# Two layernorm steps, the halved down factor and the planner's hold in a macaron block

## The chip, the cores and the metric

The kernel runs on one core of one Trainium2 chip. The metric is the device time of one execution in microseconds, as a median over runs. The engines of a core work side by side, each through its own list of instructions: TensorE (PE in the profile; its weight loads are PEld), VectorE (DVE), ScalarE (ACT), GpSimd (POOL) and SyncE (SP), which here issues nearly all DMAs.

## The reference

A macaron block in float32: half a gated feed-forward step, causal attention with rotary positions, and the same feed-forward step again. x is 4 x 1024 x 256.

```python
def ffn(x):
    g = (x @ gate_w.T) * gate_s            # 256 -> 704
    u = (x @ up_w.T) * up_s
    return ((silu(g) * u) @ down_w.T) * down_s

x = x + 0.5 * ffn(layernorm(x))
x = x + attn(layernorm(x))                 # 16 heads of 16, rotary, causal softmax
x = x + 0.5 * ffn(layernorm(x))
```

The layernorm has no weights of its own: (x - mean) / sqrt(var + 1e-5). The factor 0.5 ahead of each feed-forward step is folded into its weights.

## The kernel before

**Tiling.** The 4096 rows of x are cut into 8 blocks of 512 rows (two to a sequence), a block into 4 tiles of 128 rows. A block goes through `ffn(i, 1)`, `qkv(i)`, attention and `ffn(i, 2)`. Weights stay in SBUF; the blocks of x stay in six buffers and are updated in place.

**Layernorm.** `norm` (line 334) works on two tiles at a time. VectorE takes the statistics (L339, L342), GpSimd forms the reciprocal root (L348, L349), VectorE the shift (L352, a scalar-tensor-tensor step on two columns), and the tile itself is scaled and shifted by ScalarE (L359) or, for the second tile of each pair of the very first layernorm alone (`dve = [False, src is x0 and i == 0]`), by VectorE (L357): two VectorE tiles in the whole program. For block 0 before its first feed-forward step and its attention, and for the last block before its second feed-forward step, the tiles are then transposed on TensorE (L420) and copied out by ScalarE (L424); all others are transposed by VectorE (L391) and a trip through DRAM (L401, L407).

**Feed-forward.** 22 products of 512 columns give gate and up parts (L466, input wgu); ScalarE's tanh (L480, L500) and VectorE's two steps (L483/L486, L503/L506) give the hidden rows hT; six products for each tile (L526, with wd) go down, and VectorE adds the result to x (L532). A product in float32 is two passes in the trace, so 22 products show as 44 rows.

**The down factor.** wd is scaled on chip by ds = down_s once: `scaled_wd` (line 285) first halves ds (L288), then multiplies each of the six chunks of wd by it (L290), on VectorE, among the first block's steps.

**Fills.** At the start GpSimd writes constants into long-lived buffers (L96 in the profile, `fills` at line 292: hL, padding of wd, three kT, three nm, four va), in between the norms' small steps.

**Attention.** For each block and each pair of head groups, first the row maxima (`max_half`: products L733 into a score buffer, VectorE's mask L756 on the diagonal, and the reduction L789, or L773 where two groups share a buffer), then the maxima are transposed (L813), copied (L816) and sent as an extra row into qT (L821, DMAs on SyncE's queue), then the exponentials (`exp_half`: products L846, ScalarE's L855, GpSimd's masks L867) and the values (`weigh`: L891 into av). L733 and L846 use 16 or 17 of the array's 128 rows, a half two heads and a burst four side by side, a mode that the code calls "row"; L891 uses 32 of the columns, four heads side by side, "col"; all else is "full". Two halves, often one of maxima and one of exponentials, are issued as one *burst*; each has one of two score buffers (att), and a burst needs both free.

**The order.** Nothing is ordered by hand. `Planner` (line 44) holds every operation with an estimated time, keeps a clock for each engine, and at each `step` places the operation that could start earliest; this gives each engine its fixed list of instructions. Bursts compete with the other operations there: a burst is taken if its time, less `WAIT`, comes before that of the best other operation. Its planned time is the longer of its halves plus `CHANGE["row"]` if the mode before was another. After a burst at least `GAP` = 1.2 us of other TensorE work is planned, and values behind full work are put off by `HOLD` = 0.8.

Of the kernel before, what the change touches and what calls it, by code (L numbers as in the profile page):

```python
# [13 lines left out]
ALU = mybir.AluOpType  # L14
# [3 lines left out]
P = 128  # L18
# [25 lines left out]
class Planner:  # L44
# [1 line left out]

    ENGINES = ("pe", "dve", "act", "pool", "dma")
    GAP = 1.2
    WAIT = 0.1
    CHANGE = dict(full=0.2, row=0.2, col=0.12)  # L50
    HOLD = 0.8

# [65 lines left out]
    def step(self, burst):  # L118
        best = None
        for eng in self.ENGINES:  # L120
            for c in self.candidates(eng):
                s = max(c[0], self.busy["pe"] + 0.05) if eng == "pe" else c[0]
                if c[2].mode == "col" and self.mode == "full":
                    s += self.HOLD
                key = (s, c[1])
                if best is None or key < best[0]:
                    best = (key, c)
        b = burst()
        if b is not None:
            at = max(b[0], self.busy["pe"])  # L130
            if self.since < self.GAP:
                at += self.GAP - self.since
            key = (max(at, self.busy["pe"] + 0.05) - self.WAIT, 0)
            if best is None or key < best[0]:
                halves = b[1]
                us = max(h.us for h in halves) + (self.CHANGE["row"] if self.mode != "row" else 0.0)
                at = max(b[0], self.busy["pe"])
                for h in halves:
                    h.us = us
                    self.place(h, at)  # L140
                self.mode, self.since = "row", 0.0
                return b
        assert best is not None, "nothing can be placed"
        (s, _), (at, _, op, q) = best
        if op.eng == "pe":
            self.since += op.us
            if op.mode != self.mode:
                op.us += self.CHANGE[op.mode]
                self.mode = op.mode
        self.place(op, at)  # L150
        if q is not None:
            q.popleft()
        else:
            self.loose[op.eng].remove(op)
        return None
# [15 lines left out]
def tile_macaron(  # L171
# [12 lines left out]
    nc = tc.nc  # L184
    B, T, D = x.shape
# [46 lines left out]
    wd_sb = cpool.tile([P, NI, D], F32, name="wd_sb")  # L232
    gus_sb = cpool.tile([P, 2, NI], F32, name="gus_sb")
    ds_sb = cpool.tile([P, D], F32, name="ds_sb")
# [49 lines left out]

    def scaled_wd(c):

        if c == 0:
            nc.vector.tensor_scalar(ds_sb, ds_sb, 0.5, None, ALU.mult)  # L288
        r = slice(HALF, P) if c == NF else slice(0, P)
        nc.vector.tensor_tensor(wd_sb[r, c, :], wd_sb[r, c, :], ds_sb[r, :], ALU.mult)  # L290

    def fills():

# [16 lines left out]
    wd_loaded = Op("dma", 0.0, lambda: None)  # L310
    gu_loaded.done, wd_loaded.done = 7.5, 16.0
    wd_scaled = [Op("dve", 0.35, partial(scaled_wd, c), [wd_loaded], prio=4) for c in range(NI)]

    xb = [Buf("x") for _ in range(NBLK)]
# [19 lines left out]
    def norm(i, j, src, prio, kind):  # L334

        st, xns = Buf("st"), [Buf(kind), Buf(kind)]

        def stats(n):
            nc.vector.bn_stats(st.tile[:, 6 * n : 6 * n + 6], xb[i].tile[:, j + n, :])  # L339

        def aggr(n):
            nc.vector.bn_aggr(st.tile[:, 12 + 2 * n : 14 + 2 * n], st.tile[:, 6 * n : 6 * n + 6])  # L342

        def of_both(k):
            return st.tile[:, 12:16].rearrange("p (n k) -> p n k", k=2)[:, :, k]

        def power():
            nc.gpsimd.tensor_scalar(st.tile[:, 16:18], of_both(1), EPS, None, ALU.add)  # L348
            nc.gpsimd.tensor_tensor(st.tile[:, 18:20], st.tile[:, 16:18], mhalf, ALU.pow)  # L349

        def shift():
            nc.vector.scalar_tensor_tensor(st.tile[:, 20:22], of_both(0), -1.0, st.tile[:, 18:20], ALU.mult, ALU.mult)  # L352

        def apply(n):
            scale, bias = st.tile[:, 18 + n : 19 + n], st.tile[:, 20 + n : 21 + n]
            if dve[n]:
                nc.vector.tensor_scalar(xns[n].tile, xb[i].tile[:, j + n, :], scale, bias, ALU.mult, ALU.add)  # L357
            else:
                nc.scalar.activation(xns[n].tile, xb[i].tile[:, j + n, :], AF.Identity, bias=bias, scale=scale)  # L359


        dve = [False, src is x0 and i == 0]
        a = [
            Op("dve", 0.35, partial(stats, n), [src[i, j + n]], [st, xns[n]], [xb[i]], prio=prio) for n in range(2)
        ]
        b = [Op("dve", 0.1, partial(aggr, n), [a[n]], uses=[st], prio=prio) for n in range(2)]
        c = Op("pool", 1.0, power, b, uses=[st], prio=prio)
        d = Op("dve", 0.09, shift, [c], uses=[st], prio=prio)
        e = [
            Op(  # L370
                *(("dve", 0.35) if dve[n] else ("act", 0.55)),
                partial(apply, n),
                [d],
                uses=[st, xns[n], xb[i]],
                prio=prio,
            )
            for n in range(2)
        ]
        return a, [*b, c, d, *e], list(zip(xns, e))
# [590 lines left out]
    for blk in range(NBLK):  # L970
        aTs = [Buf("aT") for _ in range(NC)]
        for gs in ((0, 1), (2, 3)):
# [3 lines left out]
            n = len(units) // 2  # L976
# [12 lines left out]
            for i, g in enumerate(gs):  # L989
                us = list(range(n + 1)) if i == 0 else [n + 1, n, *range(n + 2, 2 * n + 1)]  # L990
# [148 lines left out]
```

## Time and profile before

| | us |
|---|---|
| median of 3 runs | 1105.46 (1105.07 to 1106.7) |
| the profiled execution, its own time | 1105.23 |
| its span in the trace | 1103.3 |
| TensorE busy | 1082.3 |
| VectorE busy | 781.7 |
| ScalarE busy | 424.6 |
| GpSimd busy | 255.9 |

The span is what the profile's instructions cover; the profiled execution's own time is 1.9 us longer. The costliest groups on TensorE are L466 (704 passes), L733 and L846 (1536 each), L526 and L891 (1536). In the rows of the profile, an x and a number at the end counts instructions, a `<-` in brackets names what ended an idle time, and times are counted from the start of the span. TensorE's first instruction starts at 7.01, its first product of the feed-forward step at 17.38; the last burst of attention is at 1050.79, and what follows is the last blocks' feed-forward step.

### The profile page before, as it was taken

How to read it: one execution, taken by the hardware profiler on the slowest of the kernel's cores; microseconds unless marked ns; L12 is line 12 of the kernel's file. 1: busy time of each engine (PE TensorE's matmuls, PEld its weight loads, DVE VectorE, ACT ScalarE, POOL GpSimd, SP SyncE). 2: the span in 40 equal slices, each digit the busy share in tenths (PEclk: the TensorE clock that was granted, in tenths of full speed). 3: DMA queues.
4: the chain of work that ended last, by engine and by line, in shares of the span. 5: the costliest groups of instructions: out<-in, count | busy, mean ns of one | idle time of the engine just before them, and what ended most of it. 6: DMA issues, size and time to landing. Idle time of an engine off the chain costs nothing.

```text
span 1103.3 us, 16669 instructions
## 1 busy us (share of the span) xinstructions
PE 1082.3 (98%) x6520; PEld 537.5 (49%) x6520; DVE 781.7 (71%) x1327; ACT 424.6 (38%) x539; POOL 255.9 (23%) x469
## 2 busy tenths in 40 slices
PE   4999999999999999999999999999999999999998
PEld 2646545444454554453544554453635544445365
DVE  6669869668687787667677796677787686675232
ACT  2314333335344344435343353344343343433530
POOL 4132521402021532301103432310214320200110
PEclk9999999999999999999999999999999999999999
DMA  8121200201102012101010011101021010010000
GB/s 274 39 58 32 49 18 20 52 25 42 37 2 58 11 30 49 30 29 48 30 49 26 15 39 28 31 20 39 1 59 30 20 49 1 22 38 20 1 20 19
DMA packets 43132, 40.32 MB, mean 37 GB/s; under 512 B 3952, under 2 KB 35760, under 8 KB 42928
## 3 DMA queue, kind: packets, MB, share of 16 engines
q1 hardware_dynamic: 42912, 39.27, 13.7%
q8 instruction: 51, 0.84, 0.3%
q14 instruction: 25, 0.20, 0.1%
q10 hardware_dynamic: 144, 0.01, 0.0%
HBM read 19.60 MB, written 15.20 MB: 32 GB/s over the span
## 4 chain that ended last, share of the span: by engine, by line
PE 93%; DVE 5%; DMA 1%; SPq 1%; issue 0%; ACT 0%; DVEq 0%
PE d L466 27%; PE att L733 21%; PE d L526 16%; PE av L891 11%; PE att L846 6%; PE d L599 5%; PE d L638 3%; PE d L951 2%; DVE nm L789 1%; DMA wqkv_sb<-in_wqkv 1%; PE d L813 1%; DVE att L756 1%; DVE nm L773 1%; DVE st L339 1%; DVE xs L391 0%
## 5 line engine op out<-in xcount | busy, mean ns | idle before, releaser
L855 ACT ACTIVATE pT<-att 128x1024 f32<-128x1024 f32 x288 | 294.0, 1024 | 482.6 <-PE att L846 482.6
L789 DVE TENSOR_REDUCE nm<-att 128x2 f32<-128x1024 f32 (+1 forms) x320 | 316.3, 1007 | 72.4 <-PE att L846 64.3
L466 PE MATMUL d<-xnT,wgu_sb 128*128 128x512 f32 x704 | 339.2, 611 | 1.2 <-ACT xnT L424 0.7
L733 PE MATMUL att<-kT,qT 16*128 16x512 f32 (+3 forms) x1536 | 316.4, 520 | 2.1 <-DVE nm L773 1.3
L846 PE MATMUL att<-qT,kT 17*128 17x512 f32 (+3 forms) x1536 | 316.4, 520 | 0.0
L867 POOL TENSOR_SCALAR_AFFINE_SELECT pT<-pT 128x256 f32<-128x256 f32 x256 | 99.9, 409 | 494.8 <-ACT pT L855 487.4
L733 PEld LDWEIGHTS att<-kT,qT 16*128 16x128 f32 x1536 | 120.9, 183 | 173.1 <-issue 59.1
L466 PEld LDWEIGHTS d<-xnT,wgu_sb 128*128 128x128 f32 x704 | 124.3, 192 | 159.9 <-issue 135.7
L526 PE MATMUL d<-wd_sb,hT 128*128 128x256 f32 x640 | 162.2, 387 | 0.0
L756 DVE TENSOR_TENSOR att<-att,causal 128x512 f32<-128x512 f32 (+1 forms) x160 | 93.4, 588 | 80.8 <-PE att L846 75.0
L891 PE MATMUL av<-pT,va 128*32 128x512 f32 (+3 forms) x1536 | 137.1, 490 | 0.0
L526 PEld LDWEIGHTS d<-wd_sb,hT 128*128 128x128 f32 x640 | 116.9, 190 | 32.8 <-issue 16.1
L846 PEld LDWEIGHTS att<-qT,kT 17*128 17x128 f32 x1536 | 119.9, 183 | 20.0 <-ACT pT L855 3.0
L503 DVE SCALAR_TENSOR_TENSOR ta<-ta,d 128x512 f32<-128x512 f32 x80 | 54.7, 683 | 53.8 <-ACT ta L500 53.0
L891 PEld LDWEIGHTS av<-pT,va 128*32 128x32 f32 x1536 | 42.7, 109 | 88.2 <-issue 72.3
L500 ACT ACTIVATE ta<-d,gus_sb 128x512 f32<-128x512 f32 x80 | 54.9, 686 | 68.4 <-PE d L466 67.3
L506 DVE SCALAR_TENSOR_TENSOR hT<-d,gus_sb,ta 128x512 f32<-128x512 f32 x80 | 59.6, 744 | 18.6 <-PE d L466 17.7
L599 PE MATMUL d<-xnT,wqkv_sb 128*128 128x512 f32 x128 | 62.6, 606 | 0.0
L610 POOL TENSOR_TENSOR qs<-qs,rope_sb 128x512 f32<-128x512 f32 x32 | 40.7, 1274 | 67.3 <-DVE qs L607 67.2
L348 POOL TENSOR_SCALAR st<-st 128x2 f32<-128x2 f32 x48 | 10.5, 219 | 151.8 <-DVE st L342 145.5
L359 ACT ACTIVATE xn<-x,st 128x256 f32<-128x256 f32 x62 | 34.2, 591 | 28.6 <-DVE st L352 28.0
L532 DVE TENSOR_TENSOR x<-d,x 128x256 f32<-128x256 f32 x64 | 26.7, 418 | 21.8 <-PE d L526 21.3
(57 smaller groups left out, 650.4 us busy)
## 6 DMA issues: line engine op xcount, KB each, us to landing
xd<-xs SPq DMA_DIRECT2D x84, 128.0 KB
xnT<-xd SPq DMA_DIRECT2D x21, 512.0 KB
kT<-qT SPq DMA_DIRECT2D x64, 64.0 KB
out<-x SPq DMA_DIRECT2D x16, 256.0 KB
x<-in_x SPq DMA_DIRECT2D x7, 512.0 KB
qT<-nmT SPq DMA_DIRECT2D x128, 2.0 KB
wgu_sb<-in_wgu SPq DMA_DIRECT2D x2, 512.0 KB
rope_sb<-in_rope SPq DMA_DIRECT2D x1, 1024.0 KB
```

The source lines that it names most:

```text
L466: nc.tensor.matmul(d.tile, wgu_sb[:, k, cols], by_tile(xnT.tile[:, k]), start=(k == 0), stop=(k == NC - 1))
L500: nc.scalar.activation(a.tile, d.tile, AF.Tanh, scale=gus_sb[:, 0, c : c + 1])
L506: nc.vector.scalar_tensor_tensor(hT[c].tile, e.tile, gus_sb[:, 1, c : c + 1], a.tile, ALU.mult, ALU.mult)
L526: nc.tensor.matmul(d.tile[:, :D], hT[c].tile[:, ts(j, P)], wd_sb[:, c, :], start=(n == 0), stop=(n == NI - 1))
L599: nc.tensor.matmul(d.tile, wqkv_sb[:, k, ts(g, P)], xnT.tile[:, k, :], start=(k == 0), stop=(k == NC - 1))
L733: nc.tensor.matmul(sc.tile[:, e, c0 : c0 + w], qT[blk].tile[r, g, ts(j, P)], kt.tile[r, g, :w], start=True, stop=True,)
L756: nc.vector.tensor_tensor(d, d, causal.unsqueeze(1).unsqueeze(1).to_broadcast([P, 2, len(masked), P]), ALU.add)
L789: nc.vector.tensor_reduce(place(g, part, j), sc.tile[:, :, c0 : c0 + w], AX.X, ALU.max, negate=True)
L846: nc.tensor.matmul(sc.tile[:, e, c0 : c0 + w], kt.tile[r, g, ts(k % NB, P)], qT[blk].tile[r, g, BLK - w :], start=True, stop=True,)
L855: nc.scalar.activation(pT.tile[:, :, :w], sc.tile[:, :, :w], AF.Exp)
L867: nc.gpsimd.affine_select(out=d, in_=d, compare_op=ALU.is_ge, fill=0.0, base=0, pattern=[[0, 2], [1, P]], channel_multiplier=-1,)
L891: nc.tensor.matmul(av.tile[ts(r, HP), BLK - w :], va[base + k // NB].tile[:, k % NB, h * VS : h * VS + HP], pTs[u, r // 2].tile[:, r % 2, ...
```

## The change

Three parts. The two VectorE tiles of the first layernorm are written as a scalar-tensor-tensor step, x times scale plus the bias column repeated along the row, in place of a tensor-scalar step with two column operands. The separate halving of ds is dropped, and each of the six scalings of wd is a scalar-tensor-tensor step, wd times 0.5 times ds. In the planner, `WAIT` depends on the mode TensorE is in, 0.3 after values and 0.1 as before elsewhere, and 0.025 is added to every burst's planned time. What is computed is the same.

```diff
     GAP = 1.2
-    WAIT = 0.1
+    WAIT = dict(full=0.1, row=0.1, col=0.3)
     CHANGE = dict(full=0.2, row=0.2, col=0.12)
...
-            key = (max(at, self.busy["pe"] + 0.05) - self.WAIT, 0)
+            key = (max(at, self.busy["pe"] + 0.05) - self.WAIT[self.mode], 0)
             if best is None or key < best[0]:
                 halves = b[1]
-                us = max(h.us for h in halves) + (self.CHANGE["row"] if self.mode != "row" else 0.0)
+                us = max(h.us for h in halves) + 0.025 + (self.CHANGE["row"] if self.mode != "row" else 0.0)
...
     def scaled_wd(c):
 
-        if c == 0:
-            nc.vector.tensor_scalar(ds_sb, ds_sb, 0.5, None, ALU.mult)
         r = slice(HALF, P) if c == NF else slice(0, P)
-        nc.vector.tensor_tensor(wd_sb[r, c, :], wd_sb[r, c, :], ds_sb[r, :], ALU.mult)
+        nc.vector.scalar_tensor_tensor(wd_sb[r, c, :], wd_sb[r, c, :], 0.5, ds_sb[r, :], ALU.mult, ALU.mult)
...
             if dve[n]:
-                nc.vector.tensor_scalar(xns[n].tile, xb[i].tile[:, j + n, :], scale, bias, ALU.mult, ALU.add)
+                nc.vector.scalar_tensor_tensor(
+                    xns[n].tile, xb[i].tile[:, j + n, :], scale, bias.to_broadcast([P, D]), ALU.mult, ALU.add
+                )
```

## The prediction

> **What bounds the kernel now.** First the shares by engine and the chain that ended last (parts 1 and 4 of the page): they say which engine is worth shortening.
>
> ```profile
> PE 1082.3 (98%) x6520; PEld 537.5 (49%) x6520; DVE 781.7 (71%) x1327; ACT 424.6 (38%) x539; POOL 255.9 (23%) x469
> ...
> PE 93%; DVE 5%; DMA 1%; SPq 1%; issue 0%; ACT 0%; DVEq 0%
> ```
>
> TensorE is the bound, and the only one: VectorE has 29% of the span free. Whatever the change does has to show as less work, less switching or less waiting on TensorE. So the next view is the list of TensorE's own waits, longest first (engine, line, releaser: total us, times, longest):
>
> ```profile
> PE d L420 <- DMA wqkv_sb<-in_wqkv: 7.3, 1, 7.3
> PE d L420 <- ACT xn L359: 7.0, 1, 7.0
> PE att L733 <- DVE nm L773: 1.3, 3, 0.5
> PE d L466 <- ACT xnT L424: 0.7, 1, 0.7
> ```
>
> Two waits of 7 us, both before the first product; under 3 us in all the rest. The timeline of the first 28 us (start, us, engine, line, what) tells what they are:
>
> ```profile
> 1.86 1.81 POOL L96 MEMSET kT<- 128x2048 f32 x1
> ...
> 2.93 0.76 DVE L282 TENSOR_SCALAR gus_sb<-gus_sb 128x6 f32<-128x6 f32 x1 [2.93 <-DMA gus_sb<-in_gus]
> ...
> 7.07 3.55 POOL L96 MEMSET kT<- 128x2048 f32 x2
> 7.16 0.16 DVE L352 SCALAR_TENSOR_TENSOR st<-st 128x2 f32<-128x2 f32 x1 [0.38 <-POOL st L349]
> ...
> 7.35 8.55 DVE L357 TENSOR_SCALAR xn<-x,st 128x256 f32<-128x256 f32 x1
> ...
> 11.71 4.04 POOL L96 MEMSET va<- 128x1148 f32 x4
> 15.96 0.29 PEld L420 LDWEIGHTS d<-ident,xn 128*128 128x128 f32 x2 [7.66 <-DVE xn L357]
> ...
> 17.38 19.05 PE L466 MATMUL d<-xnT,wgu_sb 128*128 128x512 f32 x40 [0.74 <-ACT xnT L424]
> ...
> 25.25 2.22 DVE L290 TENSOR_TENSOR wd_sb<-wd_sb,ds_sb 128x256 f32<-128x256 f32 x6
> ```
>
> The second L357 takes 8.55 us; the first, the same instruction on another tile at 6.36, took 0.41. It ends at 15.90, just after the last of GpSimd's memsets (15.75), and TensorE's transposes of that tile start at 15.96. The list above blames a weight DMA for this wait; the weight load's row names L357, and that is what stood in the way. The tiny L282 shows the same thing: 0.76 us for six columns, ending at 3.69 when the memset that began at 1.86 ends (3.67). But L352, a scalar-tensor-tensor step, runs its 0.16 us at 7.16 with a memset already started.
>
> The rest of the span is a weave. The chain of waits near the end shows its prices:
>
> ```profile
> 1030.30 1.07 PE att L846 x8
> 1031.37 2.29 PE av L891 x32
> 1033.66 1.05 PE d L466 x2
> 1034.71 1.07 PE att L846 x8
> ...
> 1070.55 18.88 PE d L466 x44
> ```
>
> In a long stretch a pass of L466 takes 18.88/44 = 0.429 us. Standing alone between bursts, two passes take 1.05, not 0.86: a stretch of full-array work costs about 0.195 us beyond its work (1.05 and 1.06 in three such places).
>
> **What the Trainium skill says.** "SBUF — State Buffer", section "Who interferes with whom": a VectorE tensor_scalar in a two-port mode needs the port pair that GpSimd uses, and whoever is second blocks fully; an instruction with two SBUF inputs outside those modes blocks only against a GpSimd instruction that reads SBUF, not one that only writes. The trace agrees: 8.55 and 0.76 us beside memsets, 0.16 for L352. "Vector Engine (DVE) Microarchitecture Reference", "Points that are easy to get wrong", says that a scalar-tensor-tensor with two SBUF sources that aren't bf16 halves throughput; the only such rows here are two columns wide, so the trace doesn't tell. "TensorEngine Tiling (Array Packing)", "Key Properties": changing the tiling mode drains TensorE; the 0.195 us agree. "TensorE: Matmul & The Clock Gate", "What's actually happening": the slow clock ends after a window whose phase isn't tied to the kernel's start; here the first four passes of L466 take 3.25 us and not 1.71.
>
> **The change part by part.**
>
> *The two layernorm tiles (L357).* Same reads and writes, other form. Nearest row for 128x256 with two SBUF inputs: L290, 0.42 us. If throughput halves it adds 256 elements at VectorE's rate, which L290 and the 512-wide L503 (0.69) put at about 0.27: 0.69. The second tile is then ready at 7.35 + 0.42 = 7.8 (8.0 at the high end). TensorE isn't free then: it runs the two transposes of tile 3 from 8.01, two take 0.49, so tile 4's start at 8.50 and not at 15.96: 7.46 us gained, and both ends of the cost are hidden by tile 3. What is late next? ScalarE's copies for tiles 1 and 2 ended at 8.82 and those for 3 and 4 follow the transposes by the same 1.42 us as now, so L466 starts at 9.92 and not 17.38. Landing records in the trace: the first piece of wgu at 5.5, the others at 7.7, 9.1 and 9.7, all before their use. Behind it everything moves 7.46 us earlier except the DMA that was running anyway: wd at 14.9 is wanted at 17.8, block 1 of x at 16.26 is wanted at 16.42 (23.88 now): a bare fit, with perhaps 0.1 us lost. GpSimd's memsets still end at 15.75; hL and the wd padding, the only ones needed early, are filled by 11.3. The cold clock I leave at its 1.5 us; 2.9 us of slow passes after 17.38 cost that, and with the phase unknown it may be one us of them (0.5 lost) or two of the page's windows, 6.8 us (3.4 lost, an estimate): -1.0 to +1.9.
>
> *The halved down factor.* L288 (0.28 us) goes, six L290 become scalar-tensor-tensor steps. At 0.42 each VectorE gains 0.28; at 0.69 it loses 1.6 - 0.3 = 1.3. They stand ahead of L503 at 27.51, and TensorE loses 0.19 us at 28.8 to 29.8 to them now (two passes 0.08 and 0.11 over). I take -0.19; the other end is +1.3.
>
> *The planner's new numbers.* 0.025 us more for a burst, and in the mode of values a burst may be up to 0.3 us late and still go ahead of other work. Neither is an instruction; both act through the order. In the compiled order of TensorE all products are still there, 288 bursts and 64 value stretches too, and nothing changes before the 96th row of that order. But the stretches of full-array work fall from 258 to 246: after values a burst follows at once 44 times, not 32. Twelve switches at 0.195: -2.3 us.
>
> What do twelve earlier bursts wait for? Both score buffers must be read out. Here is a burst with a mask, and values behind it:
>
> ```profile
> 205.95 0.59 PE L733 MATMUL att<-kT,qT 16*128 16x384 f32 x2
> ...
> 207.13 0.70 DVE L756 TENSOR_TENSOR att<-att,causal 128x512 f32<-128x512 f32 x1 [1.74 <-PE att L846]
> ...
> 207.87 1.29 DVE L789 TENSOR_REDUCE nm<-att 128x2 f32<-128x768 f32 x2
> ```
>
> The buffer is free at 209.16, 3.21 us after the burst began. Short values (1.86 us) end at 2.92: too early by 0.3. Long ones (2.29) end at 3.36: 0.15 us to spare. In the new order, six of the twelve added pairs are masked bursts before long values, four are double weight bursts before long values (ScalarE's two L855 end 3.11 to 3.17 after the burst: 0.2 to spare), and the net of two is plain bursts (2.40: half a microsecond to spare). So they fit, barely, as long as VectorE isn't in other work when the burst ends. Where it is, as at 326.5, the release comes at 3.94, 0.57 us late. I put 0.5 us of waits on the twelve; bounds 0 and 12 x 0.57 = 6.8, of which 2.5 is the most I believe. TensorE's small waits elsewhere (some 3.9 us over the usual price, summed over the stretches) may go either way by 1.5 in a new order.
>
> *Sum*, on the profiled execution's own time: 1105.23 - 7.46 - 0.19 - 2.3 + 0.5 = 1095.8. The median shown is 0.23 above that execution, so 1096.0.
>
> **The rivals.** A: all three parts as above, 1096.0, chance 0.84. Own range 1093.6 to 1098.8: the clock and the small waits at their good ends (-1.0, -1.5), or the clock at its bad end with one more us of waits.
> B: the start gains, but the hold's waits eat its gain: nearly all masked pairs wait 0.57 us and the clock or L290's slower form takes the rest; 1105.46 - 7.46 - 2.3 + 3.4 + 1.3 = 1100.4. For it: 0.15 us to spare. Against: the 32 direct pairs of now lose 0.01 us each. Chance 0.08.
> C: the new form is shut out by memsets too, and only the order gains: 1105.46 - 2.3 + 0.5 = 1103.7. For it: it has two SBUF inputs, of which one comes over the shared pair. Against: L352 at 7.16. Chance 0.04.
> D, slower: rows of maxima come late. The order of SyncE's queue is changed by the new plan too, with loads of xnT now ahead of some sends of nmT; the queue runs in order, so a load that waits for its buffer (L407 waits 92 us in all now for L466) holds back the sends behind it, and the weight bursts that need them. There are 32 rows. A mean wait of 0.3 us on each eats the 9.5 us won; at 0.4 the time is 1096.0 + 12.8 = 1108.8, and it decides from 0.3. Against: no wait of TensorE for qT is in the list. Chance 0.04.
>
> **How the numbers follow.** A change of 0.2% (2.2 us) is what measurement can tell. A and B are faster by more; C, 1.8 us below, counts as the same but for 0.01: faster 0.93, same 0.03, slower 0.04. The range is A's own, reaching to the near side of B: 1093.6 to 1099.2.
>
> **What would show it.** Right: the second tile's step under 0.7 us and ending before 8.1, TensorE's transposes of tile 4 at about 8.5, first L466 near 9.9; 246 full stretches at about 0.195; no wait over 0.6 us on score buffers. Wrong: the step ending with the memsets at 15.75 (C); rows with L733 or L846 waiting for DVE of 3 us or more in sum (B); L846 waiting for the nmT sends (D).

## The result, and the profile after

The changed kernel takes 1099.53 us in the median of 4 runs (1098.95 to 1099.74); the kernel before, timed beside it, 1106.08 (1105.07 to 1106.74, 4 runs). The ratio is 0.9941, 95% interval 0.9924 to 0.9958. It is faster, by 6.5 us. The prediction had 1096.0 with a range of 1093.6 to 1099.2: 3.5 us too low, and the time lies 0.33 above the range.

Shares by engine and the chain that ended last, of the changed kernel, as the page has them (span 1097.8, the execution's own time 1099.57):

```profile
PE 1081.8 (99%) x6520; PEld 538.2 (49%) x6520; DVE 773.2 (70%) x1326; ACT 423.5 (39%) x539; POOL 255.6 (23%) x469
...
PE 95%; DVE 3%; DMA 1%; issue 0%; ACT 0%; SPq 0%; POOL 0%; DVEq 0%; ACTq 0%
```

TensorE is busy for as long as before (1081.8 against 1082.3 us) in a span that is 5.5 us shorter. So its work, its switching and its slow passes together hardly changed; idle time went. VectorE's busy time fell by 8.5, of which 8.06 is the second tile step (8.55 to 0.49). TensorE's waits, longest first (engine, line, releaser: total us, times, longest):

```profile
PE d L420 <- ACT xn L359: 7.0, 1, 7.0
PE att L733 <- DVE nm L789: 1.5, 1, 1.5
PE att L733 <- DVE nm L773: 1.1, 3, 0.5
PE d L599 <- DMA xnT<-xd: 0.8, 1, 0.8
```

The wait of 7.3 us before the fourth tile's transposes is gone. Two waits are new: a single 1.5 us in which a burst (L733) waits for row maxima (before, this row held two waits, 0.4 in sum), and 0.8 us for a transfer of xnT. The timeline of the start (start, us, engine, line, what):

```profile
7.07 3.55 POOL L96 MEMSET kT<- 128x2048 f32 x2
...
7.36 0.49 DVE L355 SCALAR_TENSOR_TENSOR xn<-x,st 128x256 f32<-128x256 f32 x1
...
9.86 21.64 PE L466 MATMUL d<-xnT,wgu_sb 128*128 128x512 f32 x44 [0.74 <-ACT xnT L424]
```

The step that took 8.55 us takes 0.49, with the same memsets beside it, and the first product comes at 9.86 instead of 17.38. This is the gain. But look at how slowly the first products go. The stretch from the first L466 until full pace (window, its length, then busy us and count of PE, PEld, DVE, ACT, POOL, and last PEclk, DMA share, GB/s) was before:

```profile
17.40:20.30 2.90, 2.90 (x4) 1.35 (x5) 0.00 (x0) 0.00 (x0) 0.00 (x0) 1.00 1.01 374
```

and is in the changed kernel, with the stretch behind it:

```profile
9.90:14.90 5.00, 5.00 (x6) 2.15 (x7) 0.50 (x1) 0.68 (x1) 5.00 (x10) 1.00 0.95 329
14.90:18.00 3.10, 3.10 (x8) 1.33 (x7) 2.12 (x5) 0.69 (x1) 0.87 (x1) 1.00 1.05 411
```

Before, four passes went at about half pace; now six take 5.00 us, 0.83 each against 0.43 later. The 1.00 of PEclk says nothing about this stretch: the trace's record of the granted clock begins at 20.30 in the kernel before and at 14.90 in the changed kernel, just where full pace does, and the column shows 1.00 where there is no record. The pace of the passes is what gives the slow clock away. Six passes lose some 2.6 us, four lost 1.5 (1.54 by the prediction's own numbers: 3.25 - 1.71).

Where the whole difference lies, from the start-to-start times of TensorE's stretches in both profiled executions, less the pure work of their passes (sums made from the traces; the first block is all before the first burst, and its excess is also counted in us over pure work):

| us over pure work | before | after | after - before |
|---|---|---|---|
| first block | 11.76 | 5.11 | -6.65 |
| other full-array stretches (257, 245) | 57.3 | 58.2 | +0.9 |
| of these, twelve switches fewer at 0.203 | | | -2.4 |
| of these, waits over the usual price | 4.0 | 6.9 | +2.9 |
| bursts (row) | 64.9 | 65.1 | +0.2 |
| values (col) | 10.1 | 10.1 | 0 |

The two parts under the full-array row leave +0.4 of it unnamed. First block, full-array, bursts and values sum to -5.55; the two executions differ by 5.66. The start won a microsecond less than forecast, and the planner's part won nothing.

### The profile page after: what moved, and what is told of

The parts are those of the page before. It is cut to its first block, busy times and chain, and to the rows that moved or that the text cites. A ratio compares the mean times of both kernels' runs of the same rounds, so it can differ in the third digit from the quotient of the medians.

```text
span 1097.8 us, 16647 instructions
## 1 busy us (share of the span) xinstructions
PE 1081.8 (99%) x6520; PEld 538.2 (49%) x6520; DVE 773.2 (70%) x1326; ACT 423.5 (39%) x539; POOL 255.6 (23%) x469
## 4 chain that ended last, share of the span: by engine, by line
PE 95%; DVE 3%; DMA 1%; issue 0%; ACT 0%; SPq 0%; POOL 0%; DVEq 0%; ACTq 0%
PE d L466 28%; PE att L733 22%; PE d L526 16%; PE av L891 12%; PE att L846 6%; PE d L599 5%; PE d L638 3%; PE d L951 2%; PE d L813 1%; DVE nm L789 1%; DVE att L756 1%; DVE nm L773 0%; PE d L420 0%; DMA xd<-xs 0%; DVE hL L486 0%
## 5 line engine op out<-in xcount | busy, mean ns | idle before, releaser
L466 PE MATMUL d<-xnT,wgu_sb 128*128 128x512 f32 x704 | 341.1, 614 | 1.4 <-ACT xnT L424 0.7
L733 PE MATMUL att<-kT,qT 16*128 16x512 f32 (+3 forms) x1536 | 310.8, 520 | 3.2 <-DVE nm L789 1.5
L846 PE MATMUL att<-qT,kT 17*128 17x512 f32 (+3 forms) x1536 | 310.8, 520 | 0.0
L733 PEld LDWEIGHTS att<-kT,qT 16*128 16x128 f32 x1536 | 119.4, 183 | 173.1 <-issue 55.3
L466 PEld LDWEIGHTS d<-xnT,wgu_sb 128*128 128x128 f32 x704 | 124.3, 191 | 159.9 <-issue 137.5
L526 PE MATMUL d<-wd_sb,hT 128*128 128x256 f32 x640 | 162.7, 387 | 0.0
L526 PEld LDWEIGHTS d<-wd_sb,hT 128*128 128x128 f32 x640 | 116.9, 191 | 38.1 <-issue 22.6
L846 PEld LDWEIGHTS att<-qT,kT 17*128 17x128 f32 x1536 | 117.6, 183 | 20.7 <-ACT pT L855 3.0
```

The source lines that it names most:

```text
L466: nc.tensor.matmul(d.tile, wgu_sb[:, k, cols], by_tile(xnT.tile[:, k]), start=(k == 0), stop=(k == NC - 1))
L526: nc.tensor.matmul(d.tile[:, :D], hT[c].tile[:, ts(j, P)], wd_sb[:, c, :], start=(n == 0), stop=(n == NI - 1))
L733: nc.tensor.matmul(sc.tile[:, e, c0 : c0 + w], qT[blk].tile[r, g, ts(j, P)], kt.tile[r, g, :w], start=True, stop=True,)
L846: nc.tensor.matmul(sc.tile[:, e, c0 : c0 + w], kt.tile[r, g, ts(k % NB, P)], qT[blk].tile[r, g, BLK - w :], start=True, stop=True,)
```

## The experiments

Two theories for the missing 3.5 us. T1: the start is as forecast but for a longer slow clock, and the planner's new order brings waits that eat its twelve switches. T2 (the rivals): the start's gain is smaller for another reason, the new form's cost or a transfer that is late, and the planner's numbers do gain. Medians below are given with their spread and number of runs; ratios are to the kernel before, timed on the same chip, and are taken from all runs of both, so they need not be those of the medians.

**The start alone (e1_tiles).** The kernel before with only the two tile steps changed; the order of instructions on every engine stays that of before.

```diff
-                nc.vector.tensor_scalar(xns[n].tile, xb[i].tile[:, j + n, :], scale, bias, ALU.mult, ALU.add)
+                nc.vector.scalar_tensor_tensor(
+                    xns[n].tile, xb[i].tile[:, j + n, :], scale, bias.to_broadcast([P, D]), ALU.mult, ALU.add
+                )
```

> The kernel before with the two layernorm tiles alone in the new form; the order of every engine is that of before. Theory 1 (the start gains 7.5 us and gives 0.9 back to a longer cold clock; the planner's numbers are worth nothing or less): 6.6 us below before, first L466 at 9.9, full rate from about 15. Theory 2 (the planner's twelve switches gain their 2.3 us, and the start gains less than its 7.5 us): 3.5 to 4.5 us below before.

**The planner alone (e2_plan).** The kernel before with `WAIT = dict(full=0.1, row=0.1, col=0.3)`, `self.WAIT[self.mode]` and the 0.025; the tile steps stay tensor-scalar.

> The kernel before with the planner's two new numbers alone; TensorE's order is that of the changed kernel, 246 full stretches. Theory 1: 0.5 to 1.5 us above before, with the second L357 still at 8.5 us and 6 to 7 us of waits inside the stretches where before has 3.9. Theory 2: 2 us below before.

**The start and the hold, without the 0.025 (e3_tiles_wait), and the changed kernel again (e4_again).** e3 is e1 plus the `WAIT` lines.

> As e1 with the longer hold behind values, without the 0.025 us on a burst's planned time; 246 full stretches. If the hold's early bursts bring the new waits: 5.5 to 6.5 us below before, as the whole change. If the new waits come from the 0.025 us, or from chance of the order: 8 to 9 us below before.

> The changed kernel once more on the same chip as the others: 5.7 to 6.6 us below before. Theory 1 puts e1 at or up to 1 us below it; theory 2 puts e1 2 us above it.

These four ran on one chip, where the kernel before took 1106.31 (49 runs, all but four between 1105.12 and 1107.88):

| | median us (range, runs) | ratio (95%) |
|---|---|---|
| e1_tiles | 1099.29 (1097.59 to 1099.9, 14) | 0.9942 (0.9927 to 0.9956) |
| e2_plan | 1106.85 (1100.32 to 1109.6, 14) | 1.0008 (0.999 to 1.0027) |
| e3_tiles_wait | 1098.94 (1098.06 to 1100.91, 13) | 0.9953 (0.9933 to 0.9972) |
| e4_again | 1099.77 (1097.72 to 1102.14, 21) | 0.9949 (0.9938 to 0.9959) |

The tile steps alone bring 7.0 us, all that the whole change brings. The planner's numbers bring +0.5 in e2 against before, and +0.5 in e4 against e1 (where the down factor is in the difference too); e3, with the hold alone, is 0.35 below e1, and with 7.4 us below before it fell between the two ranges that were expected. None of these is a measurable change; a gain of 1.8, as forecast, would be a ratio of 0.9984, outside e2's interval. So T1 holds in its second half.

What eats the twelve switches is seen in the changed kernel. The chain of waits from 876 us on (start, us, what):

```profile
876.10 1.15 PE att L733 x15
877.25 0.02 issue
877.27 1.30 DVE att L756 x2
878.57 2.40 DVE nm L789 x4
```

The burst at 876.10 fills both score buffers and both have a mask. VectorE masks them (two steps, 1.30) and takes their maxima (four steps, 2.40): 3.70 us from the burst's end until both are free. TensorE's rows in that stretch:

```profile
876.10 1.17 PE L733 MATMUL att<-kT,qT 16*128 16x384 f32 x16
877.20 1.99 PE L951 MATMUL d<-wo_sb,aT 128*128 128x256 f32 x8
879.03 0.59 PE L526 MATMUL d<-wd_sb,hT 128*128 128x256 f32 x2
881.10 1.16 PE L733 MATMUL att<-kT,qT 16*128 16x256 f32 x16 [1.48 <-DVE nm L789]
```

Between this burst and the next, which needs both buffers again, the plan put only L951 and one piece of L526, about 2.4 us of work, where 3.85 were needed (877.25 to 881.10). The planner's own planned times have a gap there in the new order, and none at that place in the order of before. e3 has the new order's 246 stretches and this wait; e1 and e11 below, without the hold, don't. So the hold makes it, not the 0.025.

The wait can cost more than its 1.5 us. The windows behind it in e3_tiles_wait (columns as above, PEclk before the last two):

```profile
882.00:886.00 4.00, 4.00 (x15) 3.21 (x12) 3.90 (x7) 0.00 (x0) 0.00 (x0) 0.57 0.01 2
886.00:892.00 6.00, 6.00 (x32) 4.29 (x31) 3.08 (x5) 0.26 (x1) 0.00 (x0) 1.00 0.00 1
```

and in the changed kernel's profiled execution:

```profile
882.00:886.00 4.00, 4.00 (x25) 3.34 (x18) 3.73 (x5) 0.00 (x0) 0.00 (x0) 1.00 0.02 6
```

In e3 the clock falls to 0.57 over four microseconds right after the wait (the record has half clock from 882.6 to 886.0), and the products in it take 1.7 us more than their usual time; in the changed kernel it stays at 1.00. It happened in two of the five profiled executions of orders with this wait (e2, e3; not in the changed kernel, e4, e7), and at that place in none of the others. "TensorE: Matmul & The Clock Gate", "What's actually happening", in the Trainium skill, has the clock released by activity in windows of 3.4 us that run freely: 3.4 us (882.6 to 886.0) is how long it lasted here.

The record has the mean granted clock of every run, with or without a profile, and it shows how often this comes. A mean of 0.998 stands beside the two executions with the fall and beside no other profiled one. Of the kernels with this wait and no added transposes it stands beside 21 of 52 runs (the changed kernel 0 of 4, e2 5 of 14, e3 4 of 13, e4 12 of 21); of those with neither (before, e1, and e5, e6, e9 and e11 below) beside none of 97. These runs are longer: a median of 1100.45 against 1099.24 for the other nine of e4, 1100.30 against 1098.56 for the other nine of e3. So the new order pays another 1.2 to 1.7 us in four runs of ten. That the wait itself brings the slow clock is likely, but not shown: e6 below, which takes it out, changes the order with it and has five runs only, and with the transposes of e7 and e8 the 0.998 comes without it too (2 of 4 runs of e8).

**The memsets alone (e5_late_fills).** Is it the memsets that held up the second tile, or the tensor-scalar form? The kernel before, with its old forms, and the long memsets (kT, nm, va) placed by the planner after the second block's norms:

```diff
+    norms_done = Op("dma", 0.0, lambda: None)
+    norms_done.done = 26.0
...
-        filled[kind].append(Op("pool", us, f, prio=8))
+        filled[kind].append(Op("pool", us, f, [] if kind == "hL" else [norms_done], prio=8))
```

> The kernel before, its tensor-scalar form kept, but GpSimd writes the long fills (kT, nm, va) behind the second block's norms; TensorE's order is that of before. If the memsets alone held the step up: the second L357 takes 0.3 to 0.45 us, first L466 at 9.9, 6.5 to 7.5 us below before. If the form itself or another wait did: the step stays over 1 us and the time within 2 us of before.

It took 1098.84 (1097.92 to 1099.58, 5), ratio 0.9933 (0.992 to 0.9947), with the old form. (Beside e5 to e8 the kernel before took 1105.65, beside e10 and e11 1105.75, 9 runs each.) Its timeline:

```profile
7.38 0.41 DVE L359 TENSOR_SCALAR xn<-x,st 128x256 f32<-128x256 f32 x1
...
9.88 2.93 PE L468 MATMUL d<-xnT,wgu_sb 128*128 128x512 f32 x3 [0.74 <-ACT xnT L426]
```

The step that took 8.55 takes 0.41, as the first one does, once no memset runs beside it. The small step on gus_sb, 0.76 in the kernel before, takes 0.17 here. So the whole gain of the change is that the memsets no longer hold up the second tile; moving the memsets does the same. That agrees with "SBUF — State Buffer", "Who interferes with whom", in the Trainium skill, which has a tensor-scalar step in a two-port mode and a GpSimd instruction lock each other out. It also settles the form's price: 0.08 us a tile dearer (0.49 against 0.41), and hidden.

**Without the long wait (e6_no_stall).** The changed kernel with a hold of 0.15 in the other two modes; this order has 246 full stretches too, and its plan has no gap over 1 us.

```diff
-    WAIT = dict(full=0.1, row=0.1, col=0.3)
+    WAIT = dict(full=0.15, row=0.15, col=0.3)
```

> The changed kernel with the hold at 0.15 in the other two modes: still 246 full stretches, but no place where the plan itself leaves TensorE without work for over 1 us. If the one long wait near 877, and the slow clock that it can bring, eat the switches' gain: no wait over 1.2 us in the middle, no slow window there, 1.5 to 2.5 us below the changed kernel (some 1097.5). If the new waits are many small ones: within 0.5 us of it.

It took 1098.92 (1098.25 to 1099.96, 5), ratio 0.9937 (0.9924 to 0.9949). By the medians it is 0.6 to 0.85 below the changed kernel, but only 0.2 if each is set against the kernel before beside it: less than expected, and not clear of noise. TensorE's waits show why:

```profile
PE d L420 <- ACT xn L359: 7.1, 1, 7.1
PE d L599 <- DMA xnT<-xd: 1.0, 2, 0.8
PE att L733 <- DVE nm L773: 0.8, 2, 0.5
...
PE att L733 <- DVE st L350: 0.5, 1, 0.5
```

The 1.5 us are gone, and smaller ones stand in their place: waits over the usual price sum to 6.5 us, against 6.9 with the long one. Both plans with twelve switches fewer wait longer than the order of before, in every profile taken of them: some 5.5 us and more, with the slow clock's 1.7 of e2 and e3 left out, where the order of before has 4.0 to 5.3.

**A clock at full before the products (e7_warm).** The slow clock's size was the other open point. The changed kernel with 24 transposes of the identity into a PSUM tile that is free, from the moment the identity is there:

```diff
+        warm = pools["av", 0].tile([P, BLK], F32, name="av", tag="av0")
+        for n in range(24):
+            o = n % 4 * P
+            nc.tensor.transpose(warm[:, o : o + P], ident, ident)
```

> The changed kernel with 24 transposes of the identity on TensorE ahead of the first real ones, their result not read. If the slow clock at the start is a matter of how long TensorE has been at work: first L466 still at 9.9 to 10.2, at full rate from its first pass, 1.5 to 2.6 us below the changed kernel, and a narrower spread. If it ends at a fixed time after the start, or with the products' own work alone: no gain.

It took 1098.3 (1096.31 to 1100.37, 5), ratio 0.9929 (0.9917 to 0.9942). By the medians it is 1.2 to 1.5 below the changed kernel, 0.8 if each is set against the kernel before beside it; the spread didn't narrow, though that had been expected, and the intervals of the ratios overlap, so the trace carries this reading. TensorE's timeline at the start:

```profile
1.44 4.83 PE L284 MATMUL av<-ident 128*128 128x128 f32 x24 [1.44 <-POOL ident masks.py:199]
...
9.38 4.99 PE L470 MATMUL d<-xnT,wgu_sb 128*128 128x512 f32 x11 [0.74 <-ACT xnT L428]
```

Eleven passes in 4.99 us, 0.45 each, where the changed kernel's first six took 5.00; the record of full clock begins at 5.6. The first product comes 0.5 earlier too, since the transposes of x are faster. The first block's excess falls from 5.11 to 3.77. So the slow passes after 9.86 were real time on the path. Not all of the 2.6 us come back, and VectorE's and TensorE's rows show what takes part of them:

```profile
13.84 0.69 DVE L507 SCALAR_TENSOR_TENSOR ta<-ta,d 128x512 f32<-128x512 f32 x1 [0.25 <-ACT ta L504]
16.26 0.43 DVE L341 BATCH_NORM_STATS2 st<-x 128x6 f32<-128x256 f32 x1 [1.73 <-DMA x<-in_x]
16.60 0.73 DVE L510 SCALAR_TENSOR_TENSOR hT<-d,gus_sb,ta 128x512 f32<-128x512 f32 x1
...
17.39 3.70 PE L470 MATMUL d<-xnT,wgu_sb 128*128 128x512 f32 x8 [0.87 <-DVE hT L510]
```

The statistics of block 1 (L341) stand ahead of L510 in VectorE's list, and they wait for block 1 of x, which lands at 16.26, as in the kernel before. TensorE, now faster, waits for L510: 0.87 here and 1.1 in all. This is the "bare fit" of the prediction; it held in the changed kernel, where the same step came at 17.42, and no longer holds when the slow passes go.

**Both (e8_both), and the memsets with the transposes (e10_fills_warm).** e8 is e6 and e7 together. e10 is e5 and e7's lines on the kernel before, with neither the new forms nor the planner's numbers.

> e6 and e7 together: their gains add, 3 to 5 us below the changed kernel (1094.5 to 1096.5), which would put the switches' twelve gains back on the sum.

> e5 (the order and the forms of before, long fills behind) with e7's 24 transposes ahead; nothing of the planner's new numbers in it. If these are worth nothing: 1.3 to 2 us below e5, level with the changed kernel plus the same transposes (e7, 1098.3) or up to 1.5 us below it. If the switches do pay: 1 us or more above e7.

e8: 1097.02 (1095.5 to 1097.3, 4), ratio 0.9916 (0.9902 to 0.9929), the best of all, and all its runs are below every run of both kernels; it falls short of the 3 to 5 us below the changed kernel that were expected. e10: 1098.15 (1097.69 to 1098.91, 5), ratio 0.9931 (0.9919 to 0.9944), 0.7 below e5 where 1.3 to 2 were expected. e10 equals e7 without a single line of the change: once more the hold and the 0.025 as the change has them are worth nothing here. e8 is 1.3 below e7, which differs from it by e6's hold alone; whether that hold gains in earnest is open, with four and five runs and overlapping intervals.

**The kernel before once more (e9_before), and the 0.025 alone (e11_plus).** e9 is a second profile of the unchanged kernel, to see how far one execution's start stands for the others. e11 is e1 and the 0.025.

> The kernel before once more, for a second look at its slow clock. If its first profile was at the good end (full rate 2.9 us after the first L466): now 3.5 to 6 us after it, and a profiled time of 1106 to 1108. If a late start meets a shorter slow clock by rule: again 2.9 us, and 1105.2.

> e1 with 0.025 us more on a burst's planned time, the hold as before: 258 full stretches. If the new waits come with the hold: no wait over 1.2 us in the middle beyond that for xnT, and within 0.7 us of e1. If they come with the 0.025: the wait near 877 is here too.

e9's profiled execution took 1107.29. The stretch from its first L466 until full pace:

```profile
17.40:22.30 4.90, 4.90 (x6) 2.17 (x7) 0.39 (x1) 0.68 (x1) 0.00 (x0) 1.00 1.04 359
```

The same instruction order, the same first product at 17.38, and six slow passes instead of four: the slow stretch differs from one execution to the next, and the profile that the prediction was made from was at its short end. The rest of e9's excess over it is a wait of 1.0 us for xnT at 111, which comes and goes: it is in after, e1, e6, e7, e8, e9 and e10, and not in before, e2, e3, e4, e5 and e11. e11 took 1098.76 (1098.69 to 1100.37, 5), ratio 0.9941 (0.9927 to 0.9954), with 258 full stretches and no 1.5 us wait: the 0.025 alone moves nothing that can be measured.

## Why the prediction was right and wrong

**The tile steps: right in place and mechanism.** The second tile ended at 7.85 (forecast 7.8 to 8.0), and L466 came at 9.86 (forecast 9.92). A step took 0.49 to 0.52 where 0.42 was taken and 0.69 was the bound. e1 shows that nothing else of the change gains, and e5 that the memsets were the cause. Rival C, that the new form would be shut out too, is out.

**The down factor: right.** The six steps took 2.21 us against 2.22 for six L290 (VectorE's row at 18.48 in the changed kernel). The two late passes of L466 (0.08 and 0.10 over) are in before and e1 and gone in the changed kernel; 0.19 us is too little to be timed. The halved throughput that "Vector Engine (DVE) Microarchitecture Reference", "Points that are easy to get wrong", states for two SBUF sources doesn't show at this shape.

**The slow clock: a term of the sum mis-sized, by 1.0.** "The cold clock I leave at its 1.5 us" took it from one execution. Full pace came 2.9 us after the first product there, and 3.9 to 6.1 us after it in the executions with the early start that had no transposes added (5.0 in the changed kernel's), and 4.9 in e9 at the old start. So the first block gained 6.65, not 7.46 + 0.19 = 7.65. The range had allowed for it (up to +1.9); the value taken was the good end of a spread.

**The planner's numbers: the step that failed.** "Twelve switches at 0.195: -2.3 us" was right by itself: 12 stretches fewer at 0.203, -2.4. "I put 0.5 us of waits on the twelve" was enough, for the twelve. In the chain of waits of the changed kernel the direct joints, burst on values on burst, show none:

```profile
1018.28 1.07 PE att L846 x8
1019.36 2.29 PE av L891 x32
1021.65 1.07 PE att L846 x8
```

What failed is that only the twelve joints were priced. The hold acts only where a burst follows values, but all that comes after is planned anew, and the new order waits elsewhere: 1.57 us at 877 before a pair of masked bursts, 0.63 at 325, 0.45 at 964, 0.35 at 810, where before's own small waits (0.48 at 414, 0.48 at 654, 0.32 at 182 among them) are gone. The prediction named this ("may go either way by 1.5 in a new order") and took nothing for it; it was +2.9 in the profiled execution, 1.05 of it the xnT wait that comes by chance, so +1.85 of the order's own. On the medians the planner's part is +0.5 and not -1.8. The slow clock that can come after the wait at 877 is a cost that the prediction didn't have at all. It isn't in the four runs of the result, and even the nine runs of e4 without it (1099.24) only equal e1 (1099.29). Rival B had the right place (waits on score buffers), though with far too high a price and not at the joints. Rival D didn't appear: no burst waited for the maxima's transfers.

**The sum.** Forecast 1095.8 for the profiled execution, measured 1099.57, 3.8 over: 1.0 in the first block, 2.7 in the planner's part (+0.9 instead of -1.8, with the chance wait inside), 0.1 left.

## What to carry to other kernels

When one VectorE instruction of a like pair takes far longer than the other, look at what GpSimd does in the same microseconds, and either change the form or move GpSimd's work; each gave all of the gain here. When a planner's number changes, counting the switches that go is half of the sum: read the gaps in the new plan as well, above all where two masked bursts stand near each other with little between, since the work saved comes back as waits. And a term that varies from execution to execution, as the slow clock at the start does, isn't taken from one profile; when it is removed, ask what the time won will run into, as e7 ran into block 1 of x.

## What the hardware showed that was not expected

The hold-up of the second tile doesn't come in every execution. Four of the 49 runs of the kernel before on the first chip took 1098.28 to 1098.85, as if it had not occurred. None of these was profiled, but e2's profiled execution (1101.77) has such a start, with the old form:

```profile
7.07 3.69 POOL L96 MEMSET kT<- 128x2048 f32 x2
...
7.36 1.67 DVE L357 TENSOR_SCALAR xn<-x,st 128x256 f32<-128x256 f32 x1
...
10.50 2.08 PE L466 MATMUL d<-xnT,wgu_sb 128*128 128x512 f32 x2 [0.73 <-ACT xnT L424]
```

The step got in between two memsets, which together took 3.69 us instead of 3.55, and ended after 1.67 us instead of 8.55.

The new form isn't free of GpSimd either, where GpSimd reads. In e4 a GpSimd step took longer (no other L347 in any profile took over 0.72):

```profile
6.36 0.48 DVE L355 SCALAR_TENSOR_TENSOR xn<-x,st 128x256 f32<-128x256 f32 x1
6.41 1.01 POOL L347 TENSOR_TENSOR st<-st,mhalf 128x2 f32<-128x2 f32 x1
```

In the changed kernel's own profile the same L347, also at 6.41, took 0.71 and VectorE's step 0.52. In e4 it was 0.3 us later, and L466 came at 10.15. "Who interferes with whom", cited above, has a two-input VectorE step contend with a GpSimd step that reads; here either seems to pay, by 0.04 or by 0.3 us, though no run isolates it.
